# Reordering the opening of a graph layer with experts: what stands ahead of the branch, windows summed by wide matmuls, edge loads issued ahead of edge stores

## The chip, the cores and the metric

The kernel runs on one core of a Trainium2 chip. The metric is the device time of one execution in microseconds (us). TensorE is called PE, VectorE DVE, ScalarE ACT, GpSimd POOL and SyncE SP, as in the profile; a "q" behind a name means the engine's sequencer, which also issues its DMAs. Matmuls are in float32, and each one is two instructions in the counts of the profile.

## What is computed

A graph layer and a layer of experts over 6250 nodes of 256 values and 100,000 edges of 96 values. The edges come sorted by their target node `dst`. Cut to what matters:

```python
xn  = layernorm(x)                                   # 6250 x 256
s   = segment_sum(edge, dst)                         # 6250 x 96
cnt = segment_sum(1, dst)
m   = where(cnt > 0, segment_max(edge, dst), 0)
h   = concat([xn, s, m, s / max(cnt, 1), u[0]])      # 256 + 288 + 64
x   = x + xn + relu(h @ W1 + b1) @ W2 + b2           # hidden 1024
z   = layernorm(x)
# for each node: two of 16 experts by gate logits, softmax weights
moe = sum over the two: w * (relu(z @ w1[e] + b1[e]) @ w2[e] + b2[e])   # 256 -> 512 -> 256
out = x + layernorm(z + moe) * gamma + beta
```

## The kernel before, in words

**Nodes.** The 50 tiles of 125 nodes are taken in 13 groups from the last nodes to the first; group 0 has 2 tiles, every other one 4. A group goes through statistics (`stats_x` L663-671, `root_x` L676, `scale_x` L682-684), norm (`norm_x` L690), transposes through PSUM (`turn` L739/740), eight slices of the hidden layer (`hidden` L750 for the last 32 rows, L755 for the other 512, then ACT's relu L757), `output` (L763), the residual with its statistics (L768-773), the second norm, the gate, and rows scattered to DRAM for the experts. The experts and the final norm follow; they fill the time from about 885 us on.

**Edges, first way.** Groups 0 and 1 (`GW = 2`) hold nodes with few edges. For each of their nodes a "window" of the last 20 edges (`WE = 20`) in front of the node's end is gathered by one indirect DMA for each tile (`take_window` L544-548, 960 KB). To find the end, `find_block` (L471-473, ACT) counts the blocks of 250 ids that begin below the node, `take_blocks` (L475-482, DVE and POOL) gathers that block of ids, `find_edge` (L486-489, ACT) counts in it, and `bounds` (L493-504, DVE and PE) and `index_windows` (L526-542, DVE) make of it indices and 0/1 masks. `cut_window` (L551-555, ACT, 96 columns an instruction) or `cut_window_2` (L558, DVE) multiplies the window by its mask into a second buffer. That is summed for group 0 by PE (`sum_window_2` L575-578: 20 matmuls of 96 columns with the identity into PSUM) and for group 1 by DVE as a tree (`sum_window`, `over_window` L561-572); the maximum is a tree on DVE for both (`max_window` L580-583). `mask_window` (L585-592) writes the result into `at`, and `mean_window` (L594-598, ACT) adds the mean.

**Edges, second way.** From group 2 on, the edges are streamed. They are cut into seven regions (`JR`), and each of 125 x 8 lanes walks its run of edges backwards with running sums and maxima; 34 chunks of at most 3 edges a lane. A chunk (`steps` L286-320) begins a region with `mark_runs` (L236-239, from the ids `di`), then for each column either copies (ACT, L302/303, the first column of a region) or multiplies the previous column (L306/307, DVE) and joins it with the new edges (L309/310, DVE), 0.95 us each. Then the chunk's running values are stored to `rows_d` (L317, SP, 2.25 MB in two DMAs) and the chunk after next is loaded (`load_edges` L176-184, SP, 1.125 MB in two DMAs). `raw` (loads) and `rw` (running values) have two buffers each, so chunk i+2 reads into the `raw` and writes into the `rw` of chunk i. At the end of a region a chain over lanes and partitions (L372-427, DVE and PE) writes what goes on into the next lane to `carry_d` (L427, POOL). A group of nodes then gathers its rows (`take_edges` L706) and carries (`take_carry` L713), both on POOL, and joins them (L719/721, DVE).

**Order.** Every engine runs its instructions in the order in which the program lists them (`tc.manual_schedule()`). The opening is written out by hand (L1214-1248), ends with a branch on `misfit` (L1249; the body behind it, a slow way for edges that don't fit, isn't run here), and goes on by hand behind it (L1292-1325). `misfit` comes from `check_order` (L252-257: three DVE operations over 100 x 1000 ids) and `check_fit` (L259-272). From then on the order is that of slots, 12 for a group (`SLOTS`): tasks are put at slots by `at_slot` (L1085-1170), sorted, and listed (L1327-1345); between slots, chunks of the edge stream are put in by a credit of 4.6 us a slot (`SLOT`), fixed when the program is built.

**What else the steps touch.** `load_ids` (L225-230, SP) loads the ids of one region; region 0's are among the first loads, the other six regions' twelve DMAs stand ahead of SP's branch in its queue. `fill_rows` (L1172-1179, slot 7) fills 4.2 MB of expert rows from POOL's queue. `load_edges(0)` comes at the end of the hand-written part, `load_edges(1)` at slot 8. PSUM has five accumulators (`acc`), which hidden, output and the window sums share.

Of the kernel before, what the change touches and what calls it, by code (L numbers as in the profile page):

```python
# [9 lines left out]
F32 = mybir.dt.float32  # L10
# [11 lines left out]
RR = 8  # L22
GW = 2
WE = 20
JR = (6, 5, 5, 10, 21, 20, 28)
GR = (1, 1, 1, 2, 3, 2, 1)
JS = 3
# [14 lines left out]
def kernel(  # L42
# [48 lines left out]
    assert N0 == 2 and GW == 2 and WE <= RR * JS and P * GRP[GW - 1][0] <= EP * JR[0] <= ER // 2 and all(i == 1 for i in IB[:GW])  # L91

    dram = ctx.enter_context(tc.tile_pool(name="dram", bufs=1, space=DRAM))

# [130 lines left out]
    def load_ids(c):  # L225
        e0, J = REG[c]
        L, di = RR * J, dis[c]
        src = bass.AP(tensor=dst.tensor, offset=dst.offset + e0, ap=[[L, P], [1, L + 1]])
        for o, i in halves(di, src):
            nc.sync.dma_start(o, i)  # L230
# [58 lines left out]
    def steps():  # L289

        for i, (c, s, n) in enumerate(chunks):
            e0, J = REG[c]
            if s + n == J:
                mark_runs(c)
                yield 1.5, False, None
            raw, prev = raws.pop(i), prevs.pop(c, None)
            rw = rwp.tile([P, RR, JS, 2 * EF], F32, name="rw")
            bcast = [P, RR, EF]
            for j in reversed(range(n)):
                x_j, su, mx = raw[:, :, j, :], rw[:, :, j, 0:EF], rw[:, :, j, EF:]  # L300
                if prev is None:
                    nc.scalar.copy(su, x_j)  # L302
                    nc.scalar.copy(mx, x_j)
                    prev = x_j, x_j
                else:
                    nc.vector.tensor_tensor(su, prev[0], keep[c][:, :, s + j, None].to_broadcast(bcast), op=OP.mult)  # L306
                    nc.vector.tensor_tensor(mx, prev[1], bar[c][:, :, s + j, None].to_broadcast(bcast), op=OP.min)  # L307
                    yield 1.9, False, None
                    nc.vector.tensor_tensor(su, su, x_j, op=OP.add)  # L309
                    nc.vector.tensor_tensor(mx, mx, x_j, op=OP.max)  # L310
                    prev = su, mx
                    if j:
                        yield 1.9, True, None
            prevs[c] = prev
            to = rows_of(c).rearrange("(p r j) f -> p r j f", p=P, j=J)
            for o, i_ in halves(to[:, :, s:s + n], rw[:, :, :n]):
                nc.sync.dma_start(o.rearrange("p r j f -> p r (j f)"), i_.rearrange("p r j f -> p r (j f)"))  # L317
            if i + 2 < len(chunks):
                load_edges(i + 2)
            yield 1.9, True, c if s == 0 else None  # L320

    clock = [-1]
# [152 lines left out]
    def take_blocks(a, z):  # L475
        cols = slice(a, z)
        nc.vector.tensor_scalar(blk_f[:, cols], acc1[:, cols], float(NBK), 0.5, op0=OP.add, op1=OP.mult)
        nc.vector.tensor_scalar(blk_f[:, cols], blk_f[:, cols], -1.0, 0.0, op0=OP.add, op1=OP.max)
        nc.vector.tensor_copy(blk_i[:, cols], blk_f[:, cols])  # L479
        for t in reversed(range(a, z)):  # L480
            gbs_[t] = ix.tile([P, KB], I32, name="gb", bufs=5)
# [68 lines left out]

    def cut_window(g, i, k0, k1, to):  # L551

        to = cuts[to] if isinstance(to, int) else to
        for k in range(k0, k1):
            nc.scalar.activation(to[:, k, :], G[g]["win"][i][:, k, :], AF.Copy, scale=G[g]["mk"][:, i, 0, k:k + 1])

# [12 lines left out]
            nc.vector.tensor_tensor(o, w[:, 0:h, :] if n > 2 else w[:, 0, :], w[:, h:2 * h, :] if n > 2 else w[:, 1, :], op=op)  # L569
            n = h  # L570

    def sum_window(g, i, cut):
        over_window(cuts[cut], G[g]["at"][:, i, 0:EF], OP.add)

    def sum_window_2(g, i, cut):  # L575
        G[g].setdefault("pw", []).append(acc(P)[:, 0:EF])
        for k in range(WE):
            nc.tensor.matmul(G[g]["pw"][i], ident[:P, :P], cut[:, k, :], start=(k == 0), stop=(k == WE - 1))

    def max_window(g, i):  # L580
        w = G[g]["win"][i]
# [3 lines left out]
    def mask_window(g, i):  # L585
        gi = G[g]["at"][:, i, 0:2 * EF]
        j = GRP[g][0] - W0 + i
        parts = [(gi, gi, base[0][:, j, :])]
        if "pw" in G[g]:
            parts = [(gi[:, 0:EF], G[g]["pw"][i], base[0][:, j, 0:EF]), (gi[:, EF:], gi[:, EF:], base[0][:, j, EF:])]  # L590
        for o, v, b in parts:
            nc.vector.scalar_tensor_tensor(o, v, nw[:, j:j + 1], b, op0=OP.mult, op1=OP.add)

    def mean(at, rc):  # L594

# [499 lines left out]
    for g, (a, z) in enumerate(GRP):  # L1095
        B, n = SLOTS * g, z - a
        if g:
            if g > 1:
                at_slot(max(0, B - 20), take_x, g)
                at_slot(B - 14, stats_x, g, 0, cost=1.2)  # L1100
                at_slot(B - 13, stats_x, g, 1, cost=1.2)
            at_slot(B - 11, root_x, g)
            at_slot(B - 10, scale_x, g, cost=0.5)
            at_slot(B - 9, norm_x, g)
            for i in range(n):
                if g >= GW:
                    late = 3 if g == GW else 0
                    at_slot(B - 10 + late + i // 2, take_edges, region[g], g, i)
                    at_slot(B - 9 + late + i // 2, take_carry, region[g], g, i)
                else:  # L1110
                    for h in range(2):
                        at_slot(2 * i + h, cut_window, g, i, h * WE // 2, (h + 1) * WE // 2, i % 2)
                    at_slot(2 * i + 2, sum_window, g, i, i % 2, cost=2.5)
                    at_slot(2 * i + 2, max_window, g, i, cost=4.7)
                    at_slot(2 * i + 2, mask_window, g, i, cost=0.4)
                    at_slot(2 * i + 4, mean_window, g, i)
            at_slot(B - 7, keep_x, g)
            for k in range(DC):
# [37 lines left out]
    for b in range(GW, len(IB)):  # L1156
# [1 line left out]
        a, z = node_cols(b)  # L1158
        U = max(0, SLOTS * (sum(IB[:b]) - 1) - 10 - (z - a))
        for i, t in enumerate(reversed(range(a, z))):  # L1160
            at_slot(U + i, find_block, t)
            at_slot(U + i + GS + 3, find_edge, t)
        for t0 in range(z - GS, a - GS, -GS):
            t1 = t0 + GS
            at_slot(U + z - t1 + GS, take_blocks, max(t0, a), t1, cost=0.5)
        T = max(0, SLOTS * sum(IB[:b]) - 12)
        at_slot(T, bounds, b, cost=0.4)
        at_slot(T + 1, index_nodes, b, cost=4.0)
        at_slot(T + 1, counts, b, cost=1.0)
# [6 lines left out]
            nc.gpsimd.dma_start(xg_d.rearrange("(e n) d -> n e d", n=N)[h * 128:(h + 1) * 128],  # L1176
                                fill[:, None, :].to_broadcast([128, NE, DR]))

    at_slot(7, fill_rows)

    def loads_1():
        take_x(0)
# [34 lines left out]
    with tc.manual_schedule():  # L1217
# [6 lines left out]
        nc.scalar.copy(gap, eps_t[0:1])  # L1224
        nc.vector.memset(fill, 0.0)
        block_starts()
        check_order()
        for t in reversed(range(a, z)):
            find_block(t)
        take_blocks(a, z)  # L1230
        for t in reversed(range(a1, z1)):
            find_block(t)
        check_fit()
        take_blocks(z1 - 3, z1)
        global_part()
        stats_x(0, 0)
        for t in reversed(range(a, z)):
            find_edge(t)
        bounds(0)
# [3 lines left out]
        root_x(0)  # L1243
        scale_x(0)
        norm_x(0)
        take_blocks(a1, z1 - 3)
        loads_3()
        bad_v = nc.values_load(misfit[0:1, 0:1])
    with tc.If(bad_v != 0):  # L1249
# [41 lines left out]
            nc.vector.tensor_scalar(base[0][:, t, :], base[0][:, t, :], nw[:, t:t + 1], None, op0=OP.mult)  # L1291
    with tc.manual_schedule():  # L1292
        counts(0)
        for c in range(1, len(JR)):
            load_ids(c)
        for k in range(DC):
            turn(0, k)
        for t in reversed(range(a1, z1)):
            find_edge(t)
        bounds(1)  # L1300
        for i in range(z - a):
            cut = (cut_w, cut_x)[i]
            cut_window_2(0, i, WE // 2, WE, cut)
            cut_window(0, i, 0, WE // 2, cut)
            if i == 0:
                index_windows(1)
                for h in range(2):
                    for w in windows_of(rwp.tile([P, RR, JS, 2 * EF], F32, name="rw"), 2):
                        take_window(1, len(G[1].get("win", [])), w)
        for i in range(z - a):  # L1310
            sum_window_2(0, i, (cut_w, cut_x)[i])
            max_window(0, i)
            mask_window(0, i)
            mean_window(0, i)
        counts(1)
        nc.sync.dma_start(w2s, w2.rearrange("(k p) d -> p k d", p=128))
        for k in range(DC, KC + 1):
            turn(0, k)
        cuts += [cut_x, windows_of(rawp.tile([P, RR, JS, EF], F32, name="raw"), 1)[0]]
        keep_x(0)  # L1320
        load_edges(0)
        stats_x(1, 0)
        stats_x(1, 1)
        at_slot(SLOTS * (GW - 1) - 4, load_edges, 1)

        tasks.sort(key=lambda t: t[:2])
        T, credit = 0, SLOT  # L1327
# [133 lines left out]
```

## Time and profile before

| | |
|---|---|
| time, median of 3 runs | 1454.61 us (1451.48 to 1462.26) |
| the profiled execution | 1444.57 us, of which the span of the trace 1442.8 us |
| granted PE clock, mean | 0.931 |
| busy: PE, DVE, POOL, ACT | 83%, 62%, 37%, 35% of the span |
| hidden layers start: groups 0, 1, 2, 3 | 62.9, 117.4, 222.4, 278.1 us |
| windows gathered: group 0, group 1 | issued 23.3 and 24.8; 43.0 to 48.0 us |
| stream: first operation, first store issued | 131.2, 145.9 us |
| DMA, mean over the span | 203 GB/s |

Rows of a timeline have the start and the length in us, the engine, the line of the kernel, the operation, output<-inputs by the program's names, and sizes; in brackets stands the engine's idle time just ahead and what ended it. Rows of one line (for a source line) have count, shortest/median/longest in ns and the first and last start in us. Rows of windows have, for a stretch of the span, the busy time of each engine and its instructions, the granted PE clock, the DMA engines' busy share and GB/s. Rows of waits have the waiting operation, what it waited for, and the total, number and longest of these waits. Starts are from the span's beginning.

### The profile page before, as it was taken

To read this page: it belongs to the slowest core of one execution; us is meant where nothing else is said; L and a number is where in the kernel's file an instruction comes from. 1 tells how busy PE (TensorE), PEld (TensorE's weight loads), DVE (VectorE), ACT (ScalarE), POOL (GpSimd) and SP (SyncE) were. 2 spreads that over 40 slices of the span, in tenths; PEclk is the share of its full clock that TensorE was granted. 3 is DMA by queue.
4 is the path that set the end of the run, shared out by engine and by line. 5 is a ranking of instruction groups with operands and counts; after the bars stand their busy time and mean duration, and the time that the engine had idled before them with its cause. 6 is when DMAs were issued, how large, how long until landed. Compare 5 with 4: busy or idle time off the path is not lost. (4 is left out here: it accounts for less than half of the span.)

```text
span 1442.8 us, 16610 instructions
## 1 busy us (share of the span) xinstructions
PE 1191.0 (83%) x4867; PEld 843.2 (58%) x4867; DVE 900.1 (62%) x2332; ACT 510.5 (35%) x1178; POOL 527.2 (37%) x611
## 2 busy tenths in 40 slices
PE   2858258978886779898888999898999999999773
PEld 1743144635454445555445566786888888888562
DVE  4487569859785969998587333343444444444287
ACT  3384134544435543443334432321222122122133
POOL 4133033573546553373333622233333233333100
PEclk9988579989998889999989999999999999999897
DMA  6726676796868897888888323646677886666296
GB/s 183 167 62 175 181 206 187 197 235 181 228 186 255 215 268 212 241 231 221 242 216 239 87 80 104 202 169 216 224 239 246 275 272 234 219 229 222 89 275 195
DMA packets 156310, 292.28 MB, mean 203 GB/s; under 512 B 31379, under 2 KB 95652, under 8 KB 148910
## 3 DMA queue, kind: packets, MB, share of 16 engines
q1 hardware_dynamic: 119870, 234.35, 55.3%
q0 software_dynamic: 36224, 56.33, 13.8%
q8 instruction: 42, 0.69, 0.2%
q14 instruction: 62, 0.51, 0.1%
q10 hardware_dynamic: 112, 0.41, 0.1%
HBM read 169.70 MB, written 123.21 MB: 203 GB/s over the span
## 5 line engine op out<-in xcount | busy, mean ns | idle before, releaser
L755 PE MATMUL acc<-inT,w1x 128*128 128x500 f32 (+1 forms) x832 | 371.5, 598 | 0.0
L755 PEld LDWEIGHTS acc<-inT,w1x 128*128 128x128 f32 x832 | 161.8, 202 | 176.5 <-issue 174.7
L1060 POOL DMA_INDIRECT y_d<-yb,to_i x114 | 134.3, 1178 | 294.2 <-ACT yb L1059 269.1
L1041 PE MATMUL acc<-xT,wt 128*128 128x256 f32 x912 | 221.2, 385 | 7.8 <-ACT hb L1047 6.2
L1054 PE MATMUL acc<-wt,hb 128*128 128x256 f32 x912 | 209.4, 382 | 7.2 <-DVE hb L1045 7.2
L763 PE MATMUL acc<-w2s,hT 128*125 128x256 f32 x800 | 197.4, 406 | 16.5 <-ACT hT L757 16.5
L868 POOL DMA_INDIRECT xg_d<-xr,pos_i x100 | 130.2, 1302 | 217.8 <-DVE xr L864 156.4
L1054 PEld LDWEIGHTS acc<-wt,hb 128*128 128x128 f32 x912 | 173.7, 191 | 33.6 <-DVE hb L1045 9.6
L1041 PEld LDWEIGHTS acc<-xT,wt 128*128 128x128 f32 x912 | 168.1, 190 | 39.2 <-ACT hb L1047 16.9
L763 PEld LDWEIGHTS acc<-w2s,hT 128*125 128x125 f32 x800 | 160.5, 205 | 43.7 <-ACT hT L757 17.3
L1059 ACT ACTIVATE yb<-yb,xb 128x256 f32<-128x256 f32 x114 | 51.7, 500 | 349.5 <-issue 294.4
L1057 DVE TENSOR_TENSOR yb<-acc,xb 128x512 f32<-128x512 f32 x57 | 39.4, 691 | 164.7 <-PE acc L1054 164.7
L757 ACT ACTIVATE hT<-acc,c 128x500 f32<-128x500 f32 (+1 forms) x104 | 68.4, 658 | 204.9 <-PE acc L755 204.8
L482 POOL DMA_INDIRECT gb<-in_dst_dram,blk_i x50 | 70.4, 1407 | 129.7 <-DVE blk_i L479 73.4
L309 DVE TENSOR_TENSOR rw<-rw,raw 125x768 f32<-125x768 f32 x88 | 83.6, 949 | 28.9 <-DMA raw<-in_edge_dram 28.9
L306 DVE TENSOR_TENSOR rw<-rw,keep 125x768 f32<-125x768 f32 x81 | 76.7, 946 | 32.6 <-DMA rows_d<-rw 27.1
L1021 DVE COPY xT<-pT 128x512 f32<-128x512 f32 x57 | 39.3, 690 | 74.4 <-PE pT L1019 74.2
L310 DVE TENSOR_TENSOR rw<-rw,raw 125x768 f32<-125x768 f32 x88 | 83.5, 949 | 0.0
L307 DVE TENSOR_TENSOR rw<-rw,bar 125x768 f32<-125x768 f32 x81 | 82.0, 1013 | 0.0
L713 POOL DMA_INDIRECT cg<-carry_d,next_i x44 | 62.8, 1427 | 37.5 <-issue 22.3
L706 POOL DMA_INDIRECT at<-rows_d,first_i x44 | 62.4, 1418 | 36.5 <-issue 15.7
L740 ACT COPY inT<-pT 128x500 f32<-128x500 f32 (+1 forms) x65 | 36.0, 554 | 103.3 <-PE pT L739 103.1
(297 smaller groups left out, 1511.4 us busy)
## 6 DMA issues: line engine op xcount, KB each, us to landing
wt<-in_wpack_dram SPq DMA_DIRECT2D x57, 1026.0 KB
rows_d<-rw SPq DMA_DIRECT2D x27, 1440.0 KB
rows_d<-rw SPq DMA_DIRECT2D x27, 810.0 KB
raw<-in_edge_dram SPq DMA_DIRECT2D x27, 720.0 KB
xb<-xg_d SPq DMA_DIRECT2D x57, 258.0 KB
raw<-in_edge_dram SPq DMA_DIRECT2D x27, 405.0 KB
eb<-in_eb_dram SPq DMA_DIRECT2D x57, 128.0 KB
rows_d<-rw SPq DMA_DIRECT2D x7, 960.0 KB
```

The lines of the kernel that those rows point to most:

```text
L306: nc.vector.tensor_tensor(su, prev[0], keep[c][:, :, s + j, None].to_broadcast(bcast), op=OP.mult)
L307: nc.vector.tensor_tensor(mx, prev[1], bar[c][:, :, s + j, None].to_broadcast(bcast), op=OP.min)
L309: nc.vector.tensor_tensor(su, su, x_j, op=OP.add)
L310: nc.vector.tensor_tensor(mx, mx, x_j, op=OP.max)
L482: nc.gpsimd.indirect_dma_start(out=gbs_[t], out_offset=None, in_=dst_b, in_offset=IndirectOffsetOnAxis(ap=blk_i[:, t:t + 1], axis=0))
L755: nc.tensor.matmul(pH[:, :n * P], w1x[:, k, ms], inT[:, k, :n * P], start=False, stop=(k == KC - 1))
L757: nc.scalar.activation(h[:, :n * P], pH[:, :n * P], AF.Relu, bias=c1[:, m:m + 1])
L763: nc.tensor.matmul(pO, G[g]["hT"][m][:, i * P:(i + 1) * P], w2s[:, m, :], start=(m == 0), stop=(m == HC - 1))
L868: d = nc.gpsimd.indirect_dma_start(out=xg_d[:, :], out_offset=IndirectOffsetOnAxis(ap=G[g]["pos"][:, i, k:k + 1], axis=0), in_=G[g]["xr"][ ...
L1041: nc.tensor.matmul(pB[i][:, half, :], wt[:, k * FF + m * 128:k * FF + (m + 1) * 128], xT[:, k, :], start=(k == 0), stop=(k == DC - 1))
L1054: nc.tensor.matmul(pY[:, h, :], hb[:, m, h * 128:(h + 1) * 128], wt[:, W2O + m * D:W2O + (m + 1) * D], start=(m == order[0]), stop=(m == o ...
L1060: d = nc.gpsimd.indirect_dma_start(out=y_d[:, :], out_offset=IndirectOffsetOnAxis(ap=BL[b]["to"][:, h:h + 1], axis=0), in_=yb[:, h, :], in ...
```

## The change

1. `load_ids` of regions 1 to 6 goes from ahead of SP's branch to behind the second edge load, with one memset of one element of each tile on DVE.
2. `check_order` goes behind the `find_block`s and the gathers of group 1's blocks, which become one `take_blocks` call; `gb` gets a sixth buffer. Group 1's `find_edge`s come to stand ahead of the branch on ACT.
3. The four `find_block`s of group 2 and the statistics, root and scale of group 1 go ahead of the branch.
4. Behind the branch come group 1's edges, bounds, indices and its four window gathers, then group 0's transposes and cuts.
5. The sums of both groups are matmuls of 480 columns (5 edges at once, `WB = 5`), 4 a window, and then one DVE reduction 480 to 96 (`add_window`). For group 1 they come in halves between the slices of group 0's hidden layer. All cuts of group 1 go into one buffer.
6. Both edge loads 0 and 1 are issued behind group 0's part. In every chunk the load of chunk i+2 is issued ahead of the store of chunk i.
7. `fill_rows` goes from slot 7 to 4, the mean of a window and `bounds(2)` one slot earlier. Through the credits, the two ACT copies of chunk 0 come one slot earlier.

The diff, without assertions:

```diff
@@ load_ids
         L, di = RR * J, dis[c]
+        if c:
+            nc.vector.memset(di[0:1, 0:1], 0)
@@ steps
             prevs[c] = prev
+            if i + 2 < len(chunks):
+                load_edges(i + 2)
             to = rows_of(c).rearrange("(p r j) f -> p r j f", p=P, j=J)
             for o, i_ in halves(to[:, :, s:s + n], rw[:, :, :n]):
                 nc.sync.dma_start(o.rearrange("p r j f -> p r (j f)"), i_.rearrange("p r j f -> p r (j f)"))
-            if i + 2 < len(chunks):
-                load_edges(i + 2)
@@ cut_window
-        to = cuts[to] if isinstance(to, int) else to
+        to = cuts[0] if to is None else to
@@ sums
-    def sum_window(g, i, cut):
-        over_window(cuts[cut], G[g]["at"][:, i, 0:EF], OP.add)
-
-    def sum_window_2(g, i, cut):
-        G[g].setdefault("pw", []).append(acc(P)[:, 0:EF])
-        for k in range(WE):
-            nc.tensor.matmul(G[g]["pw"][i], ident[:P, :P], cut[:, k, :], start=(k == 0), stop=(k == WE - 1))
+    def sum_window(g, i, cut, half):
+
+        if half == 0:
+            G[g].setdefault("pw", []).append(acc(P)[:, 0:WB * EF])
+        n = WE // WB // 2
+        for k in range(half * n, half * n + n):
+            nc.tensor.matmul(G[g]["pw"][i], ident[:P, :P], cut[:, k * WB:(k + 1) * WB, :].rearrange("p k f -> p (k f)"),
+                             start=(k == 0), stop=(k == 2 * n - 1))
+
+    def sum_half(g, i, half):
+        sum_window(g, i, cuts[0], half)
+
+    def add_window(g, i):
+        nc.vector.tensor_reduce(G[g]["at"][:, i, 0:EF], G[g]["pw"][i].rearrange("p (k f) -> p f k", f=EF), AX.X, OP.add)
@@ mask_window
-        parts = [(gi, gi, base[0][:, j, :])]
-        if "pw" in G[g]:
-            parts = [(gi[:, 0:EF], G[g]["pw"][i], base[0][:, j, 0:EF]), (gi[:, EF:], gi[:, EF:], base[0][:, j, EF:])]
-        for o, v, b in parts:
-            nc.vector.scalar_tensor_tensor(o, v, nw[:, j:j + 1], b, op0=OP.mult, op1=OP.add)
+        nc.vector.scalar_tensor_tensor(gi, gi, nw[:, j:j + 1], base[0][:, j, :], op0=OP.mult, op1=OP.add)
@@ slots
-            at_slot(B - 11, root_x, g)
-            at_slot(B - 10, scale_x, g, cost=0.5)
+            if g > 1:
+                at_slot(B - 11, root_x, g)
+                at_slot(B - 10, scale_x, g, cost=0.5)
...
                     for h in range(2):
-                        at_slot(2 * i + h, cut_window, g, i, h * WE // 2, (h + 1) * WE // 2, i % 2)
-                    at_slot(2 * i + 2, sum_window, g, i, i % 2, cost=2.5)
-                    at_slot(2 * i + 2, max_window, g, i, cost=4.7)
+                        at_slot(2 * i + h, cut_window, g, i, h * WE // 2, (h + 1) * WE // 2, None)
+                        at_slot(2 * i + 1 + h, sum_half, g, i, h)
+                    at_slot(2 * i + 1, max_window, g, i, cost=4.7)
+                    at_slot(2 * i + 2, add_window, g, i, cost=0.9)
                     at_slot(2 * i + 2, mask_window, g, i, cost=0.4)
-                    at_slot(2 * i + 4, mean_window, g, i)
+                    at_slot(2 * i + 3, mean_window, g, i)
...
-            at_slot(U + i, find_block, t)
+            if b > GW:
+                at_slot(U + i, find_block, t)
...
-        T = max(0, SLOTS * sum(IB[:b]) - 12)
+        T = max(0, SLOTS * sum(IB[:b]) - (13 if b == GW else 12))
...
-    at_slot(7, fill_rows)
+    at_slot(4, fill_rows)
@@ ahead of the branch
         block_starts()
-        check_order()
         for t in reversed(range(a, z)):
             find_block(t)
         take_blocks(a, z)
         for t in reversed(range(a1, z1)):
             find_block(t)
+        take_blocks(a1, z1)
+        check_order()
         check_fit()
-        take_blocks(z1 - 3, z1)
         global_part()
         stats_x(0, 0)
+        for t in reversed(range(*node_cols(GW))):
+            find_block(t)
...
         norm_x(0)
-        take_blocks(a1, z1 - 3)
+        stats_x(1, 0)
+        stats_x(1, 1)
+        root_x(1)
+        scale_x(1)
@@ behind the branch
         counts(0)
-        for c in range(1, len(JR)):
-            load_ids(c)
-        for k in range(DC):
-            turn(0, k)
         for t in reversed(range(a1, z1)):
             find_edge(t)
         bounds(1)
+        index_windows(1)
+        for h in range(2):
+            for w in windows_of(rwp.tile([P, RR, JS, 2 * EF], F32, name="rw"), 2):
+                take_window(1, len(G[1].get("win", [])), w)
+        for k in range(DC):
+            turn(0, k)
         for i in range(z - a):
             cut = (cut_w, cut_x)[i]
             cut_window_2(0, i, WE // 2, WE, cut)
             cut_window(0, i, 0, WE // 2, cut)
-            if i == 0:
-                index_windows(1)
-                for h in range(2):
-                    for w in windows_of(rwp.tile([P, RR, JS, 2 * EF], F32, name="rw"), 2):
-                        take_window(1, len(G[1].get("win", [])), w)
+            for half in range(2):
+                sum_window(0, i, cut, half)
         for i in range(z - a):
-            sum_window_2(0, i, (cut_w, cut_x)[i])
             max_window(0, i)
+            add_window(0, i)
             mask_window(0, i)
             mean_window(0, i)
...
-        cuts += [cut_x, windows_of(rawp.tile([P, RR, JS, EF], F32, name="raw"), 1)[0]]
+        cuts += [cut_x]
+        for i in range(2):
+            load_edges(i)
+        for c in range(1, len(JR)):
+            load_ids(c)
         keep_x(0)
-        load_edges(0)
-        stats_x(1, 0)
-        stats_x(1, 1)
-        at_slot(SLOTS * (GW - 1) - 4, load_edges, 1)
```

More of the change, by code (lines that the diff above doesn't have):

```diff
@@ L24 @@
 WE = 20
+WB = 5
 JR = (6, 5, 5, 10, 21, 20, 28)
@@ L90 @@
     assert KR == 32 and HC % 4 == 0 and GS * P <= 512 and NT <= GS * NE and wpack.shape[1] == WROW and D == DC * 128 and GF <= 128 and EF <= 128
-    assert N0 == 2 and GW == 2 and WE <= RR * JS and P * GRP[GW - 1][0] <= EP * JR[0] <= ER // 2 and all(i == 1 for i in IB[:GW])
+    assert WE % (2 * WB) == 0 and WB * EF <= 512 and N0 == 2 and GW == 2 and WE <= RR * JS and P * GRP[GW - 1][0] <= EP * JR[0] <= ER // 2 and all(i == 1 for i in IB[:GW])
     dram = ctx.enter_context(tc.tile_pool(name="dram", bufs=1, space=DRAM))
@@ L480, in take_blocks @@
         for t in reversed(range(a, z)):
-            gbs_[t] = ix.tile([P, KB], I32, name="gb", bufs=5)
+            gbs_[t] = ix.tile([P, KB], I32, name="gb", bufs=6)
             nc.gpsimd.indirect_dma_start(out=gbs_[t], out_offset=None, in_=dst_b,
```

## The prediction

> **What bounds the kernel now.** I read the busy shares and slices first, then the timelines of the opening (0 to 225 us), then the waits of the middle.
>
> ```profile
> PE 1191.0 (83%) x4867; PEld 843.2 (58%) x4867; DVE 900.1 (62%) x2332; ACT 510.5 (35%) x1178; POOL 527.2 (37%) x611
> PE   2858258978886779898888999898999999999773
> DMA  6726676796868897888888323646677886666296
> ```
>
> PE is at 2, 5 or 2 tenths only in the first slices (36 us each): the opening is where PE waits. Busy shares don't say on what; the branch line and the line of group 0's sums do.
>
> ```profile
> L1249 SPq COMPARE_BRANCH  x1: 45/45/45, 27.8 to 27.8; - x1
> L1249 SPq EVENT_SEMAPHORE  x8: 17/17/17, 37.4 to 38.1; - x8
> ...
> L578 PEld LDWEIGHTS acc<-w2s,ident x40: 331/332/333, 41.9 to 50.0; 125*125 125x125 f32 x40
> L578 PE MATMUL acc<-w2s,ident x40: 415/417/502, 41.9 to 50.2; 125*125 125x96 f32 x40
> ```
>
> SP takes 9.6 us from its branch to its first instruction behind it (DVE 4.7, ACT 3.0), and it branches last. One window's sum is 40 instructions in 8.7 us. Then the timeline, by start, length and idle time before (DVE, PE, SP and POOL rows):
>
> ```profile
> 38.24 0.22 DVE L511 SCALAR_TENSOR_TENSOR cnt<-cnt,nf,cnt_f 125x2 f32<-125x2 f32 x1 [13.39 <-SPq L1249]
> ...
> 111.45 0.42 DVE L592 SCALAR_TENSOR_TENSOR at<-at,nw,ct 125x192 f32<-125x192 f32 x1
> ...
> 117.43 2.05 PE L750 MATMUL acc<-inT,w1r 32*128 32x500 f32 x8 [0.80 <-ACT inT L740]
> ...
> 145.87 9.66 SPq L317 DMA_DIRECT2D rows_d<-rw  x2
> 155.59 4.12 SPq L182 DMA_DIRECT2D raw<-in_edge_dram  x2
> ...
> 168.14 0.96 DVE L306 TENSOR_TENSOR rw<-raw,keep 125x768 f32<-125x768 f32 x1 [14.21 <-DMA raw<-in_edge_dram]
> ...
> 180.92 0.61 POOL L427 DMA_DIRECT2D carry_d<-ct  x1 [39.22 <-DMA raw<-in_edge_dram]
> ...
> 222.38 1.12 PE L750 MATMUL acc<-inT,w1r 32*128 32x500 f32 x8 [0.67 <-ACT inT L740]
> ```
>
> Hidden layers of groups 0, 1 and 2 start at 62.9, 117.4 and 222.4. Group 1's waits for DVE's last mask (111.45). Behind it the edge stream is the limit: the store of chunk 0 holds SP for 9.66 us, the load of chunk 2 is issued only then, DVE stands 14.21 us, and group 2 waits for what follows.
>
> ```profile
> 133.00:145.00 12.00, 10.63 (x34) 4.47 (x32) 12.00 (x15) 7.59 (x17) 5.35 (x4) 1.00 0.29 83
> 155.00:168.00 13.00, 0.00 (x0) 0.00 (x0) 0.00 (x0) 0.00 (x0) 0.00 (x0) 0.50 0.86 214
> 222.00:785.00 563.00, 472.36 (x1698) 277.31 (x1699) 455.95 (x1152) 245.33 (x526) 268.84 (x248) 0.92 0.82 224
> ```
>
> And the waits of that last stretch (us in total, times, longest):
>
> ```profile
> DVE rw L309 <- DMA raw<-in_edge_dram: 28.7, 11, 4.8
> DVE at L719 <- DMA cg<-carry_d,next_i: 28.6, 7, 9.9
> DVE rw L306 <- DMA rows_d<-rw: 27.1, 7, 6.1
> ```
>
> By stretch (busy PE, PEld, DVE, ACT, POOL; clock, DMA share, GB/s): DMA works at 0.29 before the first store and at 0.86 while every engine stands. In the middle nearly all of DVE's idle time is DMA: 28.7 us for loaded edges, 27.1 for stores to free a buffer, 28.6 for carries.
>
> **The change, part by part.** The sum is against the profiled execution (1444.6 us, span 1442.8), which lies 10.0 under the median of 1454.6.
>
> *Ahead of the branch.* The 12 id loads leave SP (17.1 to 27.1 us in the trace), so SP can branch at about 23 and be through at 27 to 33 (4.7 to 9.6 us, the rows of DVE and SP). DVE gets more. check_order's three operations (1.20 each) ran in the shadow of ACT's find_blocks (7.7 to 11.2); behind take_blocks(1), which needs the last find_block (14.6), they end at 18.5, the reduction (2.23) at 20.8, and the misfit comes near 22.1 instead of 15.5. Everything behind it, group 0's windows too, is some 6.1 later. Group 1's statistics (4 x 0.53 and 0.6) come on top: DVE branches at about 34.5 instead of 25.4. The four gathered blocks, now one take_blocks, land at 22 to 26, in time for ACT's find_edges. So DVE goes on at 39.3 (4.7 behind its branch) to 44 (9.6); I take 41.5 against 38.24. Group 0's windows, issued at 29.4 and 30.9, land by the shortest landing of a window (14.0) at 43.4 and 44.9. Both are 3 to 6 us late, and the sums have to pay for it; past about 46 the cover is gone, and hidden(0) is later one for one.
>
> *Sums of group 0.* 4 matmuls of 480 columns are 8 instructions. The 500-column rows of L755 take 0.43 us apart in clean stretches and up to 0.83 in stages of weight loads as slow as here (0.33 against 0.19): 3.4 to 6.4 us a window instead of 8.7, two windows 4.6 to 10.6 less. DVE adds two reductions 125x480 to 96 from PSUM, between 0.32 (L592, 96 wide from PSUM) and 1.15 (125x960); I take 0.6. Group 0's last mask stays at about 59.7 (59.3 before) and hidden(0) at 62.9: gain 0, bounds -4 and +5. The profile grants clock 1.00 here while weight loads take 332 ns throughout 41.9 to 58.4, so I use 6.4. The Trainium skill, page "TensorE: Matmul & The Clock Gate", section "What's actually happening", says the array runs at full rate after about 3.4 us of sustained work. By that rule a window would cost 3.4 where I take 6.4, and hidden(0) would be up to 3 us earlier; the 17 us of slow loads here speak against it.
>
> *Sums of group 1.* Before, DVE runs four trees of 2.83 and four maxima of 5.05, with one 0.36 op stretched to 3.37 beside a POOL add: 74.70 to 111.87. After, DVE has 4 x (5.05 + 0.6 + 0.42) = 24.3 and isn't the limit. Now ACT's cuts (2.7 a half window) and PE (up to 1.6 a half on top of 1.7 to 2.3 a hidden slice) pace it, through the one cut buffer: a cut of window i+1 waits for the matmuls of window i, and queued behind that cut are ACT's relus, for which PE waits in turn. Relu 7 comes at about 98.8 (97.5 before), the last sum at 104.1, the mask at 105.2, the output matmuls end at 107.8, the turns at 111.4; with bounds(2) moved ahead, hidden(1) starts at 113: **-4.4**, bounds 109.5 (-7.9) and 117.4 (0, if ACT and PE wait for each other at each half).
>
> *First chunk of the stream.* It follows hidden(1) by 13.8 and has no missing data, since load 1 is now issued at about 59, beside group 0's work, not at 106.6. So mark_runs falls at 126.8, chunk 0's eight 0.95 us operations end at 134.5, and its two ACT copies, moved ahead of a relu, end at 137.1 instead of 145.85. Then load 2 goes first: issued 137.1 to 141.2, there at about 145 by 1.15 MB at 214 GB/s and 2.5 us around. Store 0 goes out at 141.2 to 150.9. What is late next is that store: chunk 2 writes into the buffer that it reads. By bytes (3.46 MB at 214 GB/s from 137.1) it lands at 153.3; by the 8.4 us that chunk 2's load needs behind its issue, 159.3. I take 155 to 156: chunk 2 starts **12** us earlier than 168.14, bounds 9 and 15. Chain, carry_d and the gathers follow chunk 2 at the same distance, so hidden(2) starts at 210: -12, of which 4.4 is the part above, not to be counted twice.
>
> *fill_rows and bounds.* The 4.2 MB fill goes from 104-125 to about 85-105, where the DMA share in 88 to 112 is 0.33; POOL's adds and gathers there have 11 us of idle. Nothing waits: 0. Should the fill collide with the windows of group 1 (issued 45 to 50, landing 17.8 later), +3.
> The id loads, now on SP behind edge loads 0 and 1 (15.7 us of issue for load 0 in the trace), are first needed by mark_runs(1), at about 148, and group 2's nodes, queued behind them (issued at 67.0 today), by statistics at 113.8: 0. The six memsets on DVE take 0.06 each (L1174's row) beside waits.
>
> *Load before store, 31 more times.* Here the trace has both prices. A chunk's first operations, L306 and L307 (1.83 us), need the buffer freed by the store; the next two need the load. Today the load is last, and those 1.83 us lie under it. Swapped, the store is last. If both transfers together end when they do today, every stalled chunk (11 to 13) loses 1.83: +20 to +24. Where DMA is the limit the later start costs nothing, since the queue is never empty: 0. If the stalls on loads vanish and stores are no later: -28.7. The DMA share is 0.82, so the exposed part of 22 is nearest to 0.18: **+4**.
>
> *Sum.* 1444.6 - 12 + 4 = 1436.6; with the 10.0 to the median, **1446**. Experts and output are the same instructions: 0.
>
> **Rivals.**
> B. *The stream gives it back.* All stalled chunks lose the 1.83: -12 + 24 = +12, 1467. For it: waits for the buffer are already 27.1 us; against it: a DMA share of 0.82 leaves few gaps.
> C. *The loads' stalls vanish as well.* -12 - 28.7: 1414. For it: 11 waits on L309; against it: the same bytes in the same queue.
> D. *Slower: stores land later.* Each store is issued behind a load's 4.1 us on SP, and this shows wherever a chunk waits for its buffer. At n chunks the middle changes by 4.1n - 28.7; with -12 it decides from n = 10, and at 16 (of the 18 waits in the view) it gives +24.9: 1479. For it: SP's 9.66 us a store, so that issuing, not moving, may set the landing; against it: 214 to 224 GB/s, which says moving.
> E. *It doesn't do what it says.* Load 2 waits for chunk 0's copies as the store does, or the store's landing takes all of the lead; only the 4.4 us of the opening are left: 1450.
>
> **How the numbers follow.** Main case 0.48 (1446, own range 1436 to 1456), B 0.16, C 0.13, D 0.14, E 0.09. A measurement of this kernel tells about 1% from no change, that is 1440 and 1469. Faster: all of C and 0.15 of the main case, 0.28. Slower: D and 0.05 of B, 0.19. Same: 0.53. Range 1418 to 1472: it leaves out the ends of C and D, about 2 in 10.
>
> **What would show it.** DVE's first operation behind the branch at 39 to 44 and no longer released by SP; L578's successor at 8 instructions and 3.4 to 6.4 us a window; hidden(1) near 113; load 2 issued near 137 ahead of store 0; the stall at chunk 2 gone or put down to rows_d<-rw; hidden(2) near 210; in the middle, waits on raw near 0 and waits on rows_d<-rw between 27 and 80. I am wrong if hidden(1) is later than 117 (ACT, PE and the one cut buffer in lockstep), if hidden(2) has less than half the gain, or if the sum of the two waits moves by more than 15 us.

## The result, and the profile after

The changed kernel takes 1451.35 us (median of 20 runs, 1446.76 to 1466.17) against 1451.41 us for the kernel before (20 runs, 1444.55 to 1462.26): ratio 1.0009, 95% interval 0.9986 to 1.0031. This measurement cannot tell that from no change. The profiled execution took 1458.22 us, 6.9 over its median, while the one shown of before (1444.57) lay 6.8 under its own. So the two spans must not be subtracted; stages that repeat from profile to profile can be compared.

Busy times and PE's slices, from the page of the changed kernel:

```profile
PE 1201.5 (82%) x4835; PEld 836.6 (57%) x4835; DVE 895.5 (61%) x2319; ACT 511.1 (35%) x1178; POOL 530.4 (36%) x611
...
PE   1488367969786869898877999898999999999683
```

The opening is still where PE waits. Its branch line, now L1263:

```profile
L1263 SPq EVENT_SEMAPHORE  x8: 17/17/17, 26.5 to 27.0; - x8
L1263 DVEq EVENT_SEMAPHORE  x2: 21/21/21, 42.1 to 42.2; - x2
L1263 SPq COMPARE_BRANCH  x1: 45/45/45, 23.7 to 23.7; - x1
...
L1263 DVEq COMPARE_BRANCH  x1: 72/72/72, 34.2 to 34.2; - x1
```

SP is through early, as the change means it to be; but DVE branches 8.8 us later than before and then takes 7.9 us over it, not 4.7. From the timelines of DVE, PE, ACT and SP:

```profile
42.49 0.22 DVE L514 SCALAR_TENSOR_TENSOR cnt<-cnt,nf,cnt_f 125x2 f32<-125x2 f32 x1 [8.65 <-DVEq L1263]
47.65 0.23 DVE L519 TENSOR_SCALAR nw<-ne_n,nf 125x2 f32<-125x2 f32 x1 [4.46 <-issue]
...
52.64 5.35 PE L581 MATMUL acc<-w2s,ident 125*125 125x480 f32 x8 [1.79 <-ACT w2s L558]
57.83 3.38 PE L581 MATMUL acc<-xr,ident 125*125 125x480 f32 x8
69.26 1.22 PE L756 MATMUL acc<-inT,w1r 32*128 32x250 f32 x8 [0.46 <-ACT inT L746]
...
109.07 0.35 ACT L603 ACTIVATE at<-at,rc_n 125x64 f32<-125x64 f32 x1 [3.83 <-DVE at L598]
112.40 2.16 DVE L592 TENSOR_TENSOR rw<-rw,mk 125x1920 f32<-125x1920 f32 x1 [3.36 <-ACT xr L558]
124.69 2.05 PE L756 MATMUL acc<-inT,w1r 32*128 32x500 f32 x8
...
146.25 0.83 ACT L306 COPY rw<-raw 125x768 f32<-125x768 f32 x1
147.10 1.56 SPq L183 DMA_DIRECT2D raw<-in_edge_dram  x2
150.07 11.28 SPq L322 DMA_DIRECT2D rows_d<-rw  x2
168.51 0.96 DVE L309 TENSOR_TENSOR rw<-raw,keep 125x768 f32<-125x768 f32 x1 [8.77 <-DMA rows_d<-rw]
220.29 1.12 PE L756 MATMUL acc<-inT,w1r 32*128 32x500 f32 x8 [0.67 <-ACT inT L746]
```

The sums are as short as expected (5.35 and 3.38 us a window, where one took 8.7), and yet hidden(0) is 6.4 late and hidden(1) 7.3. In the pair at 109 and 112 ACT waits for DVE's mask, then DVE for ACT's cut. Load 2 leaves ahead of store 0, and chunk 2 starts where it did before (168.14): it now waits for the store. hidden(2) is 2.1 us ahead.

The waits of DVE from 220 to 800 us:

```profile
DVE rw L309 <- DMA rows_d<-rw: 76.2, 11, 10.4
DVE at L725 <- DMA cg<-carry_d,next_i: 26.0, 7, 9.9
DVE ct L385 <- DMA carry_d<-ct: 4.7, 1, 4.7
```

No wait for loaded edges is left, and the waits for stores (27.1 before) are 76.2: more than the 55.8 that both together had been.

### The profile page after: what moved, and what is told of

Read it like the earlier page. It is cut to its first block, busy times and chain, and to the rows that moved or that the text cites. A ratio compares the mean times of both kernels' runs of the same rounds, so it can differ in the third digit from the quotient of the medians.

```text
span 1456.4 us, 16537 instructions
## 1 busy us (share of the span) xinstructions
PE 1201.5 (82%) x4835; PEld 836.6 (57%) x4835; DVE 895.5 (61%) x2319; ACT 511.1 (35%) x1178; POOL 530.4 (36%) x611
## 5 line engine op out<-in xcount | busy, mean ns | idle before, releaser
L761 PE MATMUL acc<-inT,w1x 128*128 128x500 f32 (+1 forms) x832 | 377.2, 604 | 0.0
L485 POOL DMA_INDIRECT gb<-in_dst_dram,blk_i x50 | 71.1, 1423 | 118.4 <-DVE blk_i L482 52.6
L1027 DVE COPY xT<-pT 128x512 f32<-128x512 f32 x57 | 39.3, 690 | 74.3 <-PE pT L1025 74.1
L719 POOL DMA_INDIRECT cg<-carry_d,next_i x44 | 67.5, 1535 | 37.2 <-DMA carry_d<-ct 15.6
```

The source lines that it names most:

```text
L761: nc.tensor.matmul(pH[:, :n * P], w1x[:, k, ms], inT[:, k, :n * P], start=False, stop=(k == KC - 1))
```

## The experiments

Theory: three losses hide a gain of about 1%. (1) The late order check delays everything behind it. (2) The mean of a window, one slot earlier, ties ACT and DVE together. (3) Loads ahead of stores expose the store's landing at every chunk. Rivals: the wide sums and the early load gain nothing; or the stream swallows whatever the opening gains. Each of the runs x1 to x4 changes one part of the changed kernel or of the kernel before.

Starts of the hidden layers from the profiles; "middle" is from group 2 to group 12, the last. "Ratio" is to the kernel before, timed beside it.

| kernel | group 0 | group 1 | group 2 | middle | ratio (95%) |
|---|---|---|---|---|---|
| before | 62.9 | 117.4 | 222.4 | 627.2 | |
| before, second profile | 63.9 | 118.4 | 223.8 | 633.6 | |
| after | 69.3 | 124.7 | 220.3 | 643.4 | 1.0009 (0.9986-1.0031) |
| after, second profile | 67.9 | 123.2 | 219.8 | 633.4 | |
| x1_store_first | 68.7 | 124.3 | 220.8 | 630.2 | 0.9980 (0.9956-1.0004) |
| x2_load_first_only | 63.8 | 118.1 | 221.4 | 641.4 | 1.0058 (1.0033-1.0084) |
| x3_mean_later | 68.8 | 118.5 | 213.1 | 640.7 | 0.9997 (0.9971-1.0023) |
| x4_check_early | 63.3 | 119.0 | 216.0 | 633.3 | 0.9990 (0.9962-1.0017) |
| y1_three | 62.8 | 112.8 | 210.3 | 632.6 | 0.9903 (0.9865-0.9941) |
| y2_stats_behind | 60.6 | 110.5 | 209.0 | 629.7 | 0.9863 (0.9825-0.9901) |
| z1_stats_last | 57.5 | 107.3 | 205.5 | 626.9 | 0.9878 (0.9846-0.9911) |
| z2_sums1_only | 63.1 | 113.2 | 215.7 | 644.2 | 1.0038 (1.0010-1.0066) |
| z3_sums1_cost | 62.9 | 113.2 | 219.3 | 630.7 | 0.9909 (0.9876-0.9942) |
| z4_last_cost | 57.4 | 106.8 | 205.2 | 639.1 | 0.9887 (0.9855-0.9918) |

**How far one profile carries.** Both kernels were profiled a second time.

> The kernel before, unchanged, for a second profiled execution. Theory (the first profile, 7 us under the median of 20 runs, had a short middle by scatter): hidden(0), hidden(1), hidden(2) within 1.5 us of 62.9, 117.4, 222.4; from hidden(2) to the last group 630 to 637 us instead of 627. Rival (each stage repeats): 626 to 629.

> The changed kernel, unchanged, for a second profiled execution. Theory (its first profile, 7 us over the median, had a long middle by scatter): hidden(0), hidden(1), hidden(2) within 1.5 us of 69.3, 124.7, 220.3; from hidden(2) to the last group 634 to 640 us instead of 643. Rival (each stage repeats): 642 to 645.

Up to group 2 each kernel repeats within about 1.5 us; the middle does not (627.2 and 633.6; 643.4 and 633.4, just under what was expected). So a difference of 10 us between two single middles says little; means over several profiles and the times of many runs say more. Between the second profiles the changed kernel is 4.0 us late at group 0, 4.7 late at group 1 and 4.0 ahead at group 2.

**Stores ahead of loads again, and loads ahead of stores alone.**

```diff
 # x1_store_first (from after; x2_load_first_only is the reverse, from before)
-            if i + 2 < len(chunks):
-                load_edges(i + 2)
             to = rows_of(c).rearrange("(p r j) f -> p r j f", p=P, j=J)
             for o, i_ in halves(to[:, :, s:s + n], rw[:, :, :n]):
                 nc.sync.dma_start(...)
+            if i + 2 < len(chunks):
+                load_edges(i + 2)
```

> The changed kernel with one part undone: in every chunk the store is issued ahead of the load again. Theory (two effects of the order that nearly cancel): the stretch from hidden(1) to hidden(2) grows from 95.6 to about 105 us (105.0 in the kernel before), the waits for rows_d<-rw in the middle fall from 76 to about 27 us and waits on raw come back with about 29, the middle (hidden(2) to the last group's start) shortens by 10 to 16; in all about 1.451 ms minus 2 to 7 us, ratio to the kernel before 0.995 to 1.000. Rival (the longer middle of the changed profile is only the scatter of executions): only the 9 us at the stream's start are lost, ratio 1.006.

> The kernel before with one part of the change alone: the load of chunk i+2 issued ahead of the store of chunk i. Theory: hidden(1) stays at 117 us, hidden(2) comes 7 to 9 us earlier than 222.4 (213 to 215), and the middle gives 10 to 16 back by waits for rows_d<-rw of 70 to 80 us; ratio 1.001 to 1.006. Rival (the middle doesn't change): ratio 0.994.

The order of the two DMAs is hardly felt where it was meant to help: from hidden(1) to hidden(2) takes 96.5 us in x1 and 95.6 after, 103.3 in x2 and 105.0 before. The expected 105 for x1 was wrong, and so was hidden(2) at 213 to 215 for x2 (221.4). Chunk 2 of x1, from its timelines of SP and DVE:

```profile
147.07 9.70 SPq L320 DMA_DIRECT2D rows_d<-rw  x2
156.83 4.18 SPq L183 DMA_DIRECT2D raw<-in_edge_dram  x2
...
169.08 0.96 DVE L309 TENSOR_TENSOR rw<-raw,keep 125x768 f32<-125x768 f32 x1 [9.37 <-DMA raw<-in_edge_dram]
```

Store first or load first, chunk 2 starts 22.0 (x1) or 21.4 us (after) after the first of the two is issued: it needs both. The other pair has 22.3 (before) and 20.5 (x2). Most of what shortens the stretch in x1 and in the changed kernel alike is that ACT's copies of chunk 0 stand ahead of two relus. The first DMA leaves as they end (147.08 after, 145.85 before), that is 22.4 to 22.7 us behind hidden(1), where it is 28.4 before and 27.8 in x2. Of the 9.4 us between before and after, these are 6.0 and the order 0.9; the other 2.5 lie behind chunk 2, in x1 too, and what they come from is open. The copies' place was read from the traces; it was not tried alone.

In the middle the order costs. DVE's waits there in x1:

```profile
DVE rw L312 <- DMA raw<-in_edge_dram: 36.9, 11, 7.2
...
DVE rw L309 <- DMA rows_d<-rw: 26.6, 7, 7.6
DVE rw L309 <- issue: 6.7, 1, 6.7
```

And the one line of such waits in x2:

```profile
DVE rw L306 <- DMA rows_d<-rw: 76.1, 11, 12.0
```

In x1 they are 70.2 together, against 76.2 for stores alone after; in x2 76.1 against 61.3 before (28.7 + 27.1 and 5.5 of issue). The five profiles with loads first have 69.7 to 81.0 us of these waits, the nine with stores first 58.5 to 70.2. Their middles are 633 to 643, mean 638.4, with loads first, and 627 to 634, mean 630.1, in seven with stores first. That leaves out z2 and z4, in which something else moves the middle (below); with them the mean is 632.7. In the times the order costs 8.4 us when done alone (1.0058 of 1451) and gives 4 us back when undone, the latter with intervals that overlap. The rival that the middle doesn't change is out: it put x2 at 0.994.

**The mean's place.**

```diff
 # x3_mean_later, from after
-                    at_slot(2 * i + 3, mean_window, g, i)
+                    at_slot(2 * i + 4, mean_window, g, i)
```

> The changed kernel with the mean of each window of group 1 put back to slot 2i+4. Theory (ACT and DVE in lockstep: the mean waits for DVE's mask, the second half of the next cut is queued behind it on ACT, and DVE's next maximum waits for that cut): ACT's idle 2.8 to 5.3 us ahead of each mean goes, the last cut of group 1 ends at about 106 instead of 112.4, hidden(1) starts near 118.5 instead of 124.7; ratio to the kernel before 0.996 if the lead lasts, 1.000 if later waits swallow it. Rival (PE and the one cut buffer set the pace): hidden(1) stays at 124 to 125, ratio 1.001.

From x3's timelines of DVE, ACT and PE, the maximum of window 2, the mean of window 1, the maximum of window 3 and hidden(1):

```profile
94.45 2.16 DVE L592 TENSOR_TENSOR rw<-rw,mk 125x1920 f32<-125x1920 f32 x1 [0.18 <-ACT xr L558]
...
96.64 0.34 ACT L603 ACTIVATE at<-at,rc_n 125x64 f32<-125x64 f32 x1
...
104.05 2.26 DVE L592 TENSOR_TENSOR rw<-rw,mk 125x1920 f32<-125x1920 f32 x1 [3.55 <-ACT xr L558]
...
118.47 2.05 PE L756 MATMUL acc<-inT,w1r 32*128 32x500 f32 x8
```

The means wait for nothing any more (0.54, 2.75, 3.83 and 3.02 us for the four of group 1 after). The last maximum starts at 104.1 instead of 112.4, and hidden(1) is where it was expected; with one cut buffer as in the change, the stretch from hidden(0) now takes 49.7 us. The rival, PE and that buffer setting the pace, is out. The lead reaches hidden(2) (213.1).

**The order check.**

```diff
 # x4_check_early, from after
         block_starts()
+        check_order()
...
-        take_blocks(a1, z1)
-        check_order()
         check_fit()
+        take_blocks(a1, z1)
```

> The changed kernel with the order check where it was, ahead of the block search, and its reduction ahead of the gathers of group 1's blocks. Theory (the late check made everything behind it 6 us late): misfit at 15.5 us instead of 22.8, windows of group 0 issued at about 23.5 instead of 30.0, DVE's first operation behind the branch at 35 to 38 instead of 42.5, hidden(0) at 63 instead of 69.3 and hidden(1) at 118 instead of 124.7; ratio to the kernel before 0.996 if it lasts. Rival (the late resume is the branch itself, whose jump takes longer the more gathers are in flight): DVE goes on at 40 to 43 and hidden(0) gains under 2 us, ratio 1.000.

From x4's timeline of PE:

```profile
63.29 1.22 PE L756 MATMUL acc<-inT,w1r 32*128 32x250 f32 x8 [0.46 <-ACT inT L746]
```

Group 0's windows are issued at 23.7, DVE goes on behind the branch at 37.6, hidden(0) starts at 63.3 (the row above, 69.26 after) and hidden(1) at 119.0: the theory's numbers. The jump itself is hardly shorter (7.4 us for 7.9). Each of x3 and x4 gains 6 us by hidden(1), but alone they show only 2 to 3 us in the time, and the expected 0.996 lies just outside both intervals. Against the changed kernel's 1.0009, which is itself uncertain by 0.002, neither the whole 6 us nor none of it is excluded.

**All three, and two steps on.**

```diff
 # y1_three = x1_store_first + x3_mean_later + x4_check_early
 # y2_stats_behind, from y1_three (z1_stats_last: the same four lines behind keep_x(0))
         norm_x(0)
-        stats_x(1, 0)
-        stats_x(1, 1)
-        root_x(1)
-        scale_x(1)
...
         counts(1)
+        stats_x(1, 0)
+        stats_x(1, 1)
+        root_x(1)
+        scale_x(1)
```

> The changed kernel with three parts undone together: the order check early, the mean of a window at slot 2i+4, stores ahead of loads. Theory (the change hides a gain behind these three): hidden(0) at 63, hidden(1) near 112.7, hidden(2) near 208, the stretch from there to the last group 630 us as with stores first before (643 with loads first), so the last group starts near 838 instead of 849.6 in the kernel before; ratio to the kernel before 0.990 to 0.994. Rival (a lead of the opening is swallowed by the stream, since the two single repairs moved the time by 2 to 3 us where the opening gained 6): ratio 0.996 to 0.998.

> The kernel of the run before (y1_three) with group 1's statistics, root and scale put back behind the branch, behind group 0's sums. Theory (a jump over the branch body takes long only when window gathers are in flight): DVE branches at about 25 us instead of 29.8, 2 us behind the first gather's issue, and is back by about 30 (4 to 5 us of jump, as in the kernel before, instead of 7.5 to 8); the windows of group 1 are issued near 34 to 37 instead of 44, hidden(0) at 59 to 61. Rival (the jump takes 8 us on DVE whenever SP's ids are not in its way): back at 33, hidden(0) at 62 to 63. Ratio to the kernel before 0.989 to 0.994 or as y1_three.

> The kernel of the run before (y2_stats_behind) with group 1's statistics, root and scale moved on behind group 0's last transposes, where no ACT copy of a transpose is queued behind the root. Theory: PE's wait of 3.2 us ahead of the second of those transposes goes, hidden(0) at about 57.5 instead of 60.6, hidden(1) at about 107.5, all else as there; ratio to the kernel before 0.983 to 0.987. Rival (ACT's cuts for group 1 then come later by the root's wait): hidden(1) stays at 110, ratio 0.986 to 0.988.

y1 takes 0.9903 of the time before: the gain was there, and the stream doesn't swallow it. The three alone had given about 9 of these 15 us, which their intervals cover. In y2 DVE branches 5.1 us earlier; first its branch line, then the row at which DVE stands next, from y2 and from y1:

```profile
L1259 DVEq EVENT_SEMAPHORE  x2: 21/21/21, 27.7 to 27.8; - x2
...
L1259 DVEq COMPARE_BRANCH  x1: 72/72/72, 24.5 to 24.5; - x1
L1259 ACTq COMPARE_BRANCH  x1: 45/45/45, 27.5 to 27.5; - x1
L1259 ACTq EVENT_SEMAPHORE  x1: 17/17/17, 34.5 to 34.5; - x1
...
35.33 0.23 DVE L519 TENSOR_SCALAR nw<-ne_n,nf 125x2 f32<-125x2 f32 x1 [6.53 <-issue]
...
40.80 0.23 DVE L519 TENSOR_SCALAR nw<-ne_n,nf 125x2 f32<-125x2 f32 x1 [2.74 <-issue]
```

DVE jumps in 3.2 us (7.4 in y1, where it branches at 29.6), as the theory had it. But four rows on it stands 6.53 us in y2 and 2.74 in y1, so that from its branch to L519 it takes 10.8 us in y2 and 11.2 in y1. The lead of 5.5 us at L519 is the earlier branch; the shorter jump is nearly all paid back. Group 1's windows leave at 37.8 instead of 43.3, and hidden(0) comes at 60.6 instead of 62.8. z1 gains about the expected 3 us more by hidden(2); its time and y2's are not told apart. Both beat both kernels, at 0.986 to 0.988 of the time before, with intervals that end below 0.992.

**Group 1's sums alone, and what a declared cost does.**

```diff
 # z2_sums1_only, from before (sum_half as in the change, on cuts[i % 2])
-                    at_slot(2 * i + 2, sum_window, g, i, i % 2, cost=2.5)
-                    at_slot(2 * i + 2, max_window, g, i, cost=4.7)
+                        at_slot(2 * i + 1 + h, sum_half, g, i, h)
+                    at_slot(2 * i + 1, max_window, g, i, cost=4.7)
+                    at_slot(2 * i + 2, add_window, g, i, cost=0.9)
 # z3_sums1_cost, from z2; z4_last_cost: the same line, from z1
-                    at_slot(2 * i + 2, add_window, g, i, cost=0.9)
+                    at_slot(2 * i + 2, add_window, g, i, cost=2.5)
```

> The kernel before with one part of the change alone: group 1's windows summed by 480-column matmuls in halves and one reduction on DVE, with both cut buffers and the mean at slot 2i+4 as before. Theory (the wide sums of group 1 are worth the 4 to 5 us of the forecast, which the mean's place took away in the change): from hidden(0) to hidden(1) 49 to 50.5 us instead of 54.6, hidden(1) at 112 to 113.5; hidden(2) earlier by 0 to 5 since stores begin when ACT's copies are done; ratio to the kernel before 0.997 to 1.000. Rival (DVE wasn't what set hidden(1)): 54 to 55 us, ratio 1.000.

> The kernel of z2_sums1_only with one number changed: the declared cost of add_window 2.5 instead of 0.9, which is what the tree's cost was, so that the credits put the chunks of the stream between the other tasks nearly as in the kernel before. Theory (z2's lead of 6.7 us at group 2 was lost in the middle because the lower declared cost moved chunks by a step against the groups' tasks): hidden(0) to hidden(1) 50 us as in z2, hidden(2) near 216, from there to the last group 627 to 632 us as in the kernel before (z2: 644); ratio to the kernel before 0.993 to 0.997. Rival (the middle's length is scatter, or the lead is lost to DMA anyway): middle 640 to 645, ratio 1.000 to 1.004.

> The kernel of z1_stats_last with the same one number changed (declared cost of add_window 2.5 instead of 0.9), which moves its chunks a step the other way, to places like z2's in the later groups. Theory: hidden(0) to hidden(2) as in z1 (57.5, 107.3, 205.5), the middle 637 to 645 us instead of 627; ratio to the kernel before 0.994 to 1.000 (z1: 0.988). Rival (the places of the chunks don't matter): middle 625 to 630, ratio 0.985 to 0.990.

The wide sums are worth what they were meant to be: the stretch from hidden(0) to hidden(1) is 50.2 us in z2 and 50.3 in z3 instead of 54.6. But z2 is slower than the kernel before, which nobody had expected. z3 differs from it in one number that computes nothing, the cost that the planner counts for the reduction; it moves chunks by a step against the groups' tasks, and the time goes from 1.0038 to 0.9909, further than expected and with intervals far apart. z4 makes the same move from z1: its middle grows as expected (639.1 for 626.9), its time doesn't show it (0.9887 for 0.9878). So one pair shows that such a step can cost over 1%, and the other does not show it in the time; which place is the bad one is open.

A third `rw` buffer, which might shorten the waits for stores, wasn't tried.

## Why the prediction was right or wrong

Forecast 1446, measured 1451.35, inside the main case's own range of 1436 to 1456. No change that can be told was also the outcome that it held likeliest (0.53). That the number lies so near is luck: the gain of 8 us that the sum adds up to did not come. The sum started from a median of three runs (1454.61) that lay 3.2 us above the median of twenty (1451.41), and its range was wide enough to hold no gain at all. The three signs that the prediction itself named for being wrong all showed: hidden(1) is later than 117 (124.7), hidden(2) has 2.1 us of the gain of 12, and the two waits together went from 55.8 to 76.2. The errors of the terms do not cancel either: they are +6.4 us ahead of hidden(0), +5.3 from there to hidden(1), -1.8 from there to hidden(2) and +4 in the middle, 14 together. The time shows 8 to 9 of them, which the scatter of single middles allows.

- **Ahead of the branch.** DVE goes on at 42.5 (39.3 to 44 was given, 41.5 taken), and the late check is 6 to 7 us as worked out. The failed step is "hidden(0) at 62.9: gain 0, bounds -4 and +5": it is +6.4. That adds up from three rows: DVE goes on 4.3 us later; from there to its first cut (50.53) takes 8.0 us instead of 2.7; from the first cut to hidden(0) the wide sums save 3.2 (18.7 for 21.9). The middle one was put at nothing. In it DVE stands 4.46 us four rows behind its resume, which no row of before had, and bounds and indices now come ahead of the cuts. With the check early again, hidden(0) is at 63.3 (x4).
- **Sums of group 0.** 5.35 and 3.38 us, for 3.4 to 6.4 given; the 6.4 that was taken was too careful. The instructions start 0.80 us apart or more until 56.0 and 0.40 from 56.6 on, 4 us after the first (52.64). The rule of the Trainium skill (page "TensorE: Matmul & The Clock Gate", section "What's actually happening"), full rate after about 3.4 us of sustained work, was nearer here than the rows of the narrow matmuls.
- **Sums of group 1: -4.4.** In the change hidden(1) is +7.3, of which 6.4 is the late hidden(0); the stretch itself went from 54.6 to 55.4. The size was right for the sums (z2, z3: -4.3 to -4.4). What failed is that the cuts were taken to be paced by PE and the cut buffer; they were paced by the mean, in front of them on ACT, whose move one slot earlier the working passed over (x3: hidden(1) -6.2, and the stretch 49.7). The prediction's sign for this, ACT and PE in lockstep, named the wrong pair: it was ACT and DVE.
- **First chunk of the stream: -12 at hidden(2).** The stretch from hidden(1) did shorten, by 9.4 us against 7.6 forecast, but mostly for a reason that stood there as a detail, ACT's copies (6.0). The load's place gave 0.6 (x1 to after) to 1.8 us (before to x2) at chunk 2. "What is late next is that store" was right; its landing was put 3 us too early.
- **Load before store: +4.** Mis-sized: it is 8 us on the mean of middles and 8.4 in x2, between the main case and B's 24. The waits moved to the store and grew, as rivals B and D both had it. At chunk 2 both transfers end no later than before, counted from the first issue (20.5 to 22.3 us in four profiles), which is B's premise; for the other chunks no run tells B's reason from D's.
- Foreseen for chunk 0 only: that the change's smaller declared costs move the stream's chunks. Later groups were not thought of. In the changed kernel itself no harm shows (x1's middle is 630.2).

## What to carry to other kernels

A step that waits for a store and a load starts when the later one lands: putting one ahead of the other mainly chooses which wait shows. Here loads first cost 8 us; that this is because the step's first operations need only the store is the prediction's reading, not shown. When work moves ahead on an in-order engine, look for the instruction whose producer did not move with it (the mean, the order check): it holds all that is queued behind it. And where a planner places work by declared costs, a cost is part of the schedule: change it by itself and time it before the rest is judged.

## What the runs showed of the hardware

**A branch waits for its instructions, and these can wait long behind gathers.** From an engine's branch to its first row behind it, with the time since the first window gather was issued:

| kernel, engine | since the first gather | jump, us |
|---|---|---|
| y2, DVE | 1.1 | 3.2 |
| before, ACT | 1.4 | 3.0 |
| before, DVE | 2.1 | 4.7 |
| after, ACT | 3.6 | 7.6 |
| y2, ACT | 4.1 | 7.0 |
| after, DVE | 4.2 | 7.9 |
| before, SP | 4.5 | 9.6 |
| y1, DVE | 6.2 | 7.4 |

The rows scatter: in four profiles with the same opening (after twice, x1, x3) ACT's jump is 5.6 to 7.6 us and DVE's 7.0 to 7.9. PE's takes 0.4 in all. SP's 5.6 us in y1 (17.8 to 23.4), ahead of any window gather, show that these are not the only cause.

The Trainium skill (page "Runtime: NRT & Kernel Launch", section "Instruction fetch mechanics") says that a taken branch whose target lies outside the two pages at hand must fetch the page by DMA first. The traces agree in time, since they list the DMA packets of instructions, 8 KB each. In the changed kernel none runs from 32.0 to 39.2 us, while window gathers move 1.08 MB. Two run at 39.2 and 39.8, and DVE goes on at 42.1. Its stall of 4.46 us ends 1.56 us behind the end of a later packet (46.1). In y2 a packet at 25.6 comes just ahead of DVE's short jump's end (27.7), the next two come at 32.6 and 33.2, and the stall of 6.53 us ends 1.64 us behind the second. In all nine profiles with this stall it ends 1.2 to 1.6 us behind the end of such a packet. And in none of the 14 profiles does one start between 4.6 and 7.4 us behind the issue of the first window gather: an engine that branches then waits. The traces don't say which engine a packet is for, so this is agreement in time; why the packets wait is not shown.

**Narrow matmuls stayed slow.** In the kernel before, the 80 instructions of 96 columns (two windows) ran with weight loads of 332 ns for 17 us on end; with 480 columns the loads fell from 335 to 187 ns after 4 us, in the same place and at the same granted clock of 1.00. Why the narrow ones stayed slow was not tried.
